# Gates and second shift and scale of an adaptive layer norm block, computed as columns on VectorE in place of products on TensorE

## Chip, core and metric

The kernel runs on one core of a Trainium2 chip. The metric is the device time of one execution in microseconds (us); the profile of one further execution shows where it goes. Everything is computed in float32.

## What is computed

Two samples of 1024 tokens and width 256 pass through one transformer block whose layer norms and residuals are modulated by a condition `c` (2 x 256):

```python
mod = (silu(c) @ wmod).reshape(2, 6, 1, 256)
sa, ca, ga, sb, cb, gb = (mod[:, i] for i in range(6))
ga = (2 * (ga >= 0) - 1) * maximum(abs(ga), 0.25)      # gb likewise
h = layernorm(x) * (1 + ca) + sa
x = x + ga * attention(h)       # 16 heads of 128, biases, rotary, causal softmax, Wo, bo
h = layernorm(x) * (1 + cb) + sb
x = x + gb * ffn(h)             # silu(gate) * up, 704 wide, weights dequantized, then down
```

So for each sample `wmod` gives six vectors of 256: shift, scale and gate of the attention block (`sa`, `ca`, `ga`) and of the feed-forward block (`sb`, `cb`, `gb`). The change touches how `ga`, `gb`, `sb` and `cb` are made. `sa` and `ca` are made as before.

## The kernel before

**Units and steps.** The main loop runs over 32 units, that is, heads: 16 heads of sample 0, then 16 of sample 1, two heads to a group (b, g, h). A unit n has eight steps i, one per row block of 128 tokens. The text calls unit n "head n". The order of the work on each engine is the order of the program, written out by hand under `manual_schedule`; each engine takes its instructions in order, and semaphores hold it up where it needs another's result.

In step i of head n the program issues: output products `py` of an earlier head (`shared_out`, lines 696 to 698, 13 row blocks behind) and their addition to `x` on VectorE (L521); the scores `ps` of row block i (L431) and, on VectorE, their masked negative maximum (L434, a fused add and minimum with an accumulator); the transposition of the row block before on VectorE (`turned`, L465), after every fourth of which SP issues 16 transfers `pT<-t` (L477); the exponential on ScalarE (L451); `release()`, which lets VectorE finish a half of the next head's q or k (L404). Then come, by step: projections of q and k for the next head (`project_qk`, L388, steps 1, 3, 4, 5), the values products of this group or the next (`project_v`, `pv`, L370, steps 0 and 2: two row blocks of 128 tokens each), the product of probabilities and values for the head before (`values`, `po`, L492; its first half at step 0, for heads 0 and 1 at step 2, its second half at steps 6 and 7), and `extras`, work that falls to particular steps.

**Values products.** A group's eight row blocks are made in four calls of `project_v`. For the first group all four lie in the prologue and in head 0. For every later group the first two calls lie in the second head of the group before, and the last two in its own first head. Their result goes through a PSUM tile and a ScalarE copy (L377).

**Buffers.** In PSUM, pool `ps_a` has two buffers (q and k projections, values products), `ps_o` one (`po`, values products of head 0), `ps_y` one (`py`, and of what concerns the change `pg` and the second `pm`), `ps_sc` two (scores). A q or k buffer in `ps_a` is free when ScalarE has read it (L400) and VectorE has finished L404, which is released a step later. In SBUF, `t32` holds the transposed blocks from which the 16 `pT<-t` transfers of a half are sent; VectorE can't overwrite a half before they have landed.

**Modulation.** `modulation(which, ...)` (L117) makes shift and scale of one block on TensorE: the weights are stationary, silu(c), repeated over 128 columns, is moving, and the results are columns (the 256 features on partitions), which is how they are needed. Block 0's runs at the start, block 1's at the end of step 7 of head 0 (L648). `shift_scale` (L136) copies them to `modT`, and adds 1 to the scale.

**Gates.** They are needed as rows, repeated over all partitions: `ga` is multiplied into the weights Wo of each group by GpSimd (`fold_out`, L332, first at the end of head 0), `gb` into the scales of the down projection (`ffn_down_scale`, head 8). `gates_product` (L146) multiplies silu(c), as stationary operand of two columns, with 512 columns of `wga`, in two calls of 256 inputs' halves in the prologue (L736 and L746). `gates` (L151), at L748 in the prologue, makes sign and magnitude of two rows of 512 on VectorE, writes them to DRAM (`grow_d`, two rows of 2 KB), and loads them back four times, repeated over 128 partitions.

**Queues.** SP issues nearly all transfers, in the program's order; a transfer that waits holds up those behind it. In the prologue it loads x, `wmod` for block 0, `wga`, the first weights, rotary tables, the rest of x, `wmod` for block 1, and the next group's weights. GpSimd's queue carries one transfer, `bo_bc`.

## Time and profile before

| what | before |
|---|---|
| median of 3 runs | 1075.6 us (1075.38 to 1075.73) |
| profiled execution, own time | 1076.84 us |
| its span | 1075.1 us |
| TensorE busy | 1070.5 us, 3529 instructions |
| VectorE busy | 655.1 us |
| ScalarE busy | 507.7 us |
| GpSimd busy | 396.1 us |
| DMA of SP and ACT queues | 49.4% and 1.2% of 16 engines' span |
| main loop begins, head 1, head 2, head 3 (first score on TensorE) | 25.11, 44.97, 72.54, 101.81 us |

Matmuls are pipelined, so a matmul's own duration is longer than its pitch, the time from its start to the next one's; TensorE's cost of a product is read from starts. An fp32 product takes two passes, which the trace shows as two instructions each. In the profile's groups and timelines a bracket or a last column names the idle time ahead of an instruction and what ended it. The chain of waits, followed back from the last instruction, says which engine the end of the run waited for.

### The profile page before, as it was taken

What the parts mean: (1) busy time and instruction counts of PE and PEld (TensorE: products, weight loads), DVE (VectorE), ACT (ScalarE), POOL (GpSimd) and SP (SyncE); (2) the same over time, 40 slices, a digit from 0 to 9 for tenths busy, and PEclk for the clock granted to TensorE, in tenths of its full rate; (3) what the DMA queues carried; (4) which work ended last, traced back from release to release, by engine and by line L of the source; (5) the groups of instructions that cost most, each with busy time, mean ns of one, the idle gap of its engine ahead of it and who ended that gap; (6) DMA issues with size and microseconds to landing.
All of it is one profiled execution on the core that took longest, in us unless ns stands there. A gap on an engine that the chain in (4) does not pass through costs nothing.

```text
span 1075.1 us, 12364 instructions
## 1 busy us (share of the span) xinstructions
PE 1070.5 (100%) x3529; PEld 641.4 (60%) x3529; DVE 655.1 (61%) x1423; ACT 507.7 (47%) x956; POOL 396.1 (37%) x364
## 2 busy tenths in 40 slices
PE   9999999999999999999999999999999999999998
PEld 5656555666666655555666656655555666555656
DVE  5656665666767776665666566666677765544421
ACT  4654544554445544544554444444454554562110
POOL 3825353534343343754332443324343433100000
PEclk9999999999999999999999999999999999999999
DMA  6465655657565555565554656454555556432001
GB/s 218 96 161 126 161 119 135 164 127 181 118 152 112 142 117 134 122 149 126 112 148 109 147 113 155 101 139 99 139 114 126 143 128 137 103 69 49 20 20 40
DMA packets 66656, 130.99 MB, mean 122 GB/s; under 512 B 18806, under 2 KB 22010, under 8 KB 66588
## 3 DMA queue, kind: packets, MB, share of 16 engines
q1 hardware_dynamic: 64804, 125.78, 49.4%
q10 hardware_dynamic: 1736, 4.29, 1.2%
q8 instruction: 29, 0.48, 0.2%
q14 instruction: 39, 0.32, 0.1%
q0 software_dynamic: 48, 0.13, 0.1%
HBM read 25.26 MB, written 2.10 MB: 25 GB/s over the span
## 4 chain that ended last, share of the span: by engine, by line
PE 99%; DMA 0%; DVE 0%; SPq 0%; issue 0%
PE po L492 23%; PE ps L431 23%; PE pv L370 10%; PE pq L388 10%; PE py L518 10%; PE pk L388 10%; PE pgu L547 7%; PE pd L606 3%; PE pm L125 1%; DMA wmod<-in_wmod 0%; PE pd L596 0%; PE ptx_a L218 0%; PE pg L149 0%; PE ptx_b L218 0%; PE pd_11r L606 0%; DVE x L521 0%
## 5 line engine op out<-in xcount | busy, mean ns | idle before, releaser
L451 ACT ACTIVATE p<-ps,nmax 128x128 f32<-128x128 f32 (+7 forms) x256 | 189.8, 741 | 342.7 <-DVE nmax L434 342.3
L431 PE MATMUL ps<-kT,qT 128*128 128x512 f32 (+3 forms) x768 | 289.5, 486 | 0.0
L434 DVE CUSTOM_DVE_ANT_0 ps<-ps,mask 128x128 f32<-128x128 f32 (+7 forms) x256 | 195.5, 764 | 114.5 <-PE ps L431 113.6
L492 PE MATMUL po<-pT,v 128*128 128x512 f32 (+3 forms) x768 | 263.7, 486 | 0.1
L521 DVE SCALAR_TENSOR_TENSOR x<-py,rden,x 128x256 f32<-128x256 f32 x256 | 122.7, 481 | 220.6 <-PE py L518 216.8
L492 PEld LDWEIGHTS po<-pT,v 128*128 128x128 f32 x768 | 145.7, 190 | 123.9 <-issue 92.8
L401 POOL TENSOR_TENSOR r_q<-r_q,sin_t 128x512 f32<-128x512 f32 x64 | 81.9, 1280 | 364.5 <-ACT r_q L400 348.9
L465 DVE STREAM_TRANSPOSE t<-p 128x128 f32<-128x128 f32 (+7 forms) x256 | 198.2, 774 | 3.6 <-DMA pT<-t 1.8
L431 PEld LDWEIGHTS ps<-kT,qT 128*128 128x128 f32 x768 | 145.7, 190 | 77.6 <-issue 64.1
L518 PE MATMUL py<-wo,o 128*128 128x256 f32 x512 | 151.2, 380 | 0.0
L518 PEld LDWEIGHTS py<-wo,o 128*128 128x128 f32 x512 | 92.6, 190 | 77.6 <-issue 53.1
L370 PE MATMUL pv<-wv,hT 128*128 128x256 f32 x512 | 121.1, 379 | 0.0
L388 PE MATMUL pq<-hT,wq 128*128 128x512 f32 x256 | 120.5, 593 | 0.0
L388 PE MATMUL pk<-hT,wk 128*128 128x512 f32 x256 | 120.3, 592 | 0.0
L370 PEld LDWEIGHTS pv<-wv,hT 128*128 128x128 f32 x512 | 94.8, 190 | 19.5 <-issue 1.3
L401 POOL TENSOR_TENSOR r_k<-r_k,sin_t 128x512 f32<-128x512 f32 x64 | 81.5, 1273 | 64.4 <-ACT r_k L400 64.4
L407 POOL TENSOR_TENSOR kT<-kT,r_k 128x512 f32<-128x512 f32 x64 | 81.2, 1269 | 55.8 <-DVE kT L404 41.1
L400 ACT ACTIVATE r_q<-pq,cols 64x512 f32<-64x512 f32 x128 | 87.4, 683 | 22.3 <-PE pq L388 19.8
L407 POOL TENSOR_TENSOR qT<-qT,r_q 128x512 f32<-128x512 f32 x64 | 83.7, 1308 | 33.9 <-DVE qT L404 29.7
L400 ACT ACTIVATE r_k<-pk,cols 64x512 f32<-64x512 f32 x128 | 87.4, 683 | 6.4 <-PE pk L388 1.0
L388 PEld LDWEIGHTS pk<-hT,wk 128*128 128x128 f32 x256 | 48.6, 190 | 48.0 <-issue 44.2
L388 PEld LDWEIGHTS pq<-hT,wq 128*128 128x128 f32 x256 | 46.2, 190 | 33.1 <-issue 30.6
(96 smaller groups left out, 691.3 us busy)
## 6 DMA issues: line engine op xcount, KB each, us to landing
pT<-t SPq DMA_DIRECT2D x512, 128.0 KB, 2.4
pT<-t SPq DMA_DIRECT2D x512, 64.0 KB, 2.0
wq<-in_Wq SPq DMA_DIRECT2D x16, 256.0 KB, 3.0
wk<-in_Wk SPq DMA_DIRECT2D x16, 256.0 KB, 4.1
wv<-in_Wv SPq DMA_DIRECT2D x16, 256.0 KB, 4.1
wo<-in_Wo SPq DMA_DIRECT2D x16, 256.0 KB, 2.9
out<-yo SPq DMA_DIRECT2D x15, 128.0 KB, 1.8
wmod<-in_wmod SPq DMA_DIRECT2D x4, 256.0 KB, 5.5
```

Source lines behind the costliest of these rows:

```text
L370: nc.tensor.matmul(pv[:, ts(j, HG * DH)], hT[b, n][:, k, ts(r, P)], weights[b, g]["v"][:, k, :], start=(k == 0), stop=(k == KC - 1),)
L388: nc.tensor.matmul(pq, weights[b, g][s][:, k, ts(h, DH)], hT[b, n][:, k, :], start=(k == 0), stop=(k == KC - 1),)
L400: nc.scalar.activation(r1[to], pq[of], AF.Identity, bias=cols[of, c : c + 1])
L401: nc.gpsimd.tensor_tensor(r1, r1, sin_t[:, sl], ALU.mult)
L407: nc.gpsimd.tensor_tensor(dst[:, sl], dst[:, sl], r1, ALU.add)
L431: nc.tensor.matmul(ps[:, c:e], qT[:, ts(i, P)], kT[:, c:e], start=True, stop=True)
L434: nc.vector.tensor_tensor_reduce(ps[:, :L], ps[:, :L], mask[:, NT - 1 - i :, :].rearrange("p t k -> p (t k)"), -SCALE, FLT_MAX, ALU.add, A ...
L451: nc.scalar.activation(p[:, :L], ps[:, :L], AF.Exp, bias=nmax, scale=-1.0, accum_out=dens[u][:, i : i + 1])
L465: nc.vector.transpose(t32[blk][:, :, j, : i + 1, :].rearrange("p c k b -> p k c b"), p[:, : (i + 1) * P].rearrange("p (k c a) -> p k c a", ...
L492: nc.tensor.matmul(po[:, off * P :], vs[b, g][:, k, ts(h, DH)], pT[:, off:, :, k, :], start=(k == 0), stop=(k == last),)
L518: nc.tensor.matmul(py[:, :D], outs[u][:, ts(t, P)], weights[b, g]["o"][:, h, :], start=True, stop=True)
L521: nc.vector.scalar_tensor_tensor(x[b][:, t, :], py[:, :D], rdens[u][:, t : t + 1], x[b][:, t, :], ALU.mult, ALU.add)
```

## The change

- `gates_product`, its weights `wga` and their load are gone, and so is the modulation of block 1 on TensorE. `modulation` now serves block 0 alone; it is called after `ln_scale`, and includes its two copies to `modT`.
- In their place `late_mod`, one buffer of the same pool, holds `wmT` (the weights of both gates and of block 1's shift and scale, transposed: output features on partitions, the 256 inputs along the row, 1 MB in two loads at the place of block 1's `wmod`) and `crow` (silu(c) of both samples as rows, repeated over all partitions).
- `crow` comes about at the start: ScalarE applies Silu to the row `row_c`, GpSimd's queue writes it to DRAM and loads it back repeated over the partitions.
- `column(which, n, f)` makes 128 features for both samples by one fused product and sum on VectorE each (`tensor_tensor_reduce` over 256 elements), into `gcol` or `modT`. `extras` calls it at steps 1 to 4 of head 0 (gates) and of head 1 (block 1's shift and scale): sixteen fused products in all.
- `gates` then works on 128 x 8 elements in place of 2 x 512, and moves from the prologue to step 4 of head 0. It writes its columns to `grow_d` so that they become rows there, and loads the rows back as before.
- The values products of the second group are all made in the first two heads: the first two calls at steps 6 and 7 of head 0, the other two at steps 0 and 2 of head 1. Head 2 has none. Later groups are as before.
- The first half of `values` moves from step 0 to step 2 in head 2, too.

```diff
-    wmod = fpool.tile([P, 2, 2, KC, D], F32, tag="f", name="wmod")
-    wga = fpool.tile([P, KC, 2 * D], F32, tag="f", name="wga")
+
+    wmod = fpool.tile([P, 2, KC, D], F32, tag="f", name="wmod")
+    late_mod = fpool.tile([P, (4 * KC + B) * D], F32, tag="f", name="late_mod")
+    wmT = late_mod[:, : 4 * KC * D].rearrange("p (w n f k) -> p w n f k", w=2, n=2, f=KC)
+
+    crow = late_mod[:, 4 * KC * D :].rearrange("p (b k) -> p b k", b=B)
...
-    def gates_product(k):
-        if k == 0:
-            pgs.append(ps_y.tile([P, 512], F32, tag="y", name="pg"))
-        nc.tensor.matmul(pgs[0][:B], sc[:, :, k], wga[:, k, :], start=(k == 0), stop=(k == KC - 1))
+    crow_d = dram.tile([1, B * D], F32, name="crow_d")
+    grow_d = dram.tile([B, 2, KC, P], F32, name="grow_d")
+    gcol = const.tile([P, B, 2, KC], F32, name="gcol")
+
+    def column(which, n, f):
+
+        junk = xnp.tile([P, D], F32, tag="xn", name=f"junk{which}{n}{f}")
+        for b in range(B):
+            to = modT[:, 2 + n, f, b : b + 1] if which else gcol[:, b, n, f : f + 1]
+            nc.vector.tensor_tensor_reduce(
+                junk, wmT[:, which, n, f], crow[:, b], 1.0, float(which * n), ALU.mult, ALU.add, to
+            )
 
     def gates():
 
-        pg = pgs.pop()
-        sgn = ppool.tile([P, S], F32, tag="p", name="sgn")[:B, :QB]
-        nc.vector.tensor_scalar(sgn, pg[:B], 0.0, 2.0, ALU.is_ge, ALU.mult)
...
+        g = gcol.rearrange("p b n f -> p (b n f)")
+        sgn = small.tile([P, 4 * B], F32, tag="sgn", name="sgn", bufs=1)
+        nc.vector.tensor_scalar(sgn, g, 0.0, 2.0, ALU.is_ge, ALU.mult)
...
-        nc.sync.dma_start(grow_d, mag)
+        with nc.allow_non_contiguous_dma("columns to rows"):
+            nc.sync.dma_start(grow_d.rearrange("b n f p -> p (b n f)"), mag)
         for b in range(B):
             for m, n in enumerate(("a", "b")):
                 nc.sync.dma_start(
-                    gate[n, b], grow_d[b : b + 1, m * D : (m + 1) * D].to_broadcast([P, D])
+                    gate[n, b],
+                    grow_d[b : b + 1, m].rearrange("b f p -> b (f p)").to_broadcast([P, D]),
                 )
...
-        if n == 0 and i == 7:
-            modulation(2, ps_y, "y")
-            shift_scale(2)
+
+        if n < 2 and 1 <= i <= 4:
+            column(n, *divmod(i - 1, 2))
+        if n == 0 and i == 4:
+            gates()
...
         nc.scalar.activation(sc.rearrange("p b k -> p (b k)"), pc[:, : B * KC], AF.Silu)
+        nc.scalar.activation(row_c, row_c, AF.Silu)
+        nc.gpsimd.dma_start(crow_d.rearrange("o (r p) -> (o r) p", p=P), row_c)
+        nc.gpsimd.dma_start(
+            crow.rearrange("p b k -> p (b k)"), crow_d.to_broadcast([P, B * D])
+        )
         nc.scalar.activation(warm, eps_t, AF.Sqrt)
         weights[0, 0] = {}
-        nc.sync.dma_start(wga, a["w_gates"])
...
         for n in range(2):
-            load_wmod(1, n, nc.sync)
+            nc.sync.dma_start(wmT[:, n], a["wmodT"][:, n])
...
-        modulation(0, ps_o, "o")
         ln_scale(0, "a", 0, (0, 1))
         ln_scale(0, "a", 0, (2, 3))
-        shift_scale(0)
+        modulation(ps_o, "o")
         ln_turn(0, "a", 0, 0, new_hT(0, 0), split=True)
-        gates_product(0)
...
         ln_turn(0, "a", 1, 0, new_hT(0, 1), split=True, wide=True)
-        gates_product(1)
         project_v(0, 0, 2, ps_sc, "sc", S)
-        gates()
...
+
                 if i in (0, 2):
-                    if h == 0:
-                        project_v(b, g, 4 + i, *((ps_a, "a") if n else (ps_o, "o")))
-                    elif more:
+                    if n < 2:
+                        project_v(b, n, 4 + i, *((ps_a, "a") if n else (ps_o, "o")))
+                    elif h == 0 and n > 2:
+                        project_v(b, g, 4 + i)
+                    elif h and more:
                         project_v(nb, ng, i)
+                if n == 0 and i in (6, 7):
+                    project_v(0, 1, 2 * (i - 6))
...
-                if prev and i == (0 if n > 1 else 2):
+                if prev and i == (0 if n > 2 else 2):
                     values(prev, 0, 0, 4)
```

More of the change, by code (lines that the diff above doesn't have):

```diff
@@ L58, in adaln_block, with load_wmod @@
     sc = const.tile([P, B, KC], F32, name="sc")
-    wmod = fpool.tile([P, 2, 2, KC, D], F32, tag="f", name="wmod")
-    wga = fpool.tile([P, KC, 2 * D], F32, tag="f", name="wga")
+    wmod = fpool.tile([P, 2, KC, D], F32, tag="f", name="wmod")
+    late_mod = fpool.tile([P, (4 * KC + B) * D], F32, tag="f", name="late_mod")
+    wmT = late_mod[:, : 4 * KC * D].rearrange("p (w n f k) -> p w n f k", w=2, n=2, f=KC)
+    crow = late_mod[:, 4 * KC * D :].rearrange("p (b k) -> p b k", b=B)
     def load_x(b, t, n, eng):
         eng.dma_start(x[b][:, t : t + n, :], x_d[b, :, t : t + n, :])
-    def load_wmod(block, n, eng):
-        eng.dma_start(wmod[:, block, n], a["L0_wmod"][block, n])
+    def load_wmod(n, eng):
+        eng.dma_start(wmod[:, n], a["L0_wmod"][n])
     row_c = rot.tile([P, QB], F32, tag="r1", name="row_c")[: B * KC, :P]
@@ L76, in adaln_block @@
     for n in range(2):
-        load_wmod(0, n, nc.sync)
+        load_wmod(n, nc.sync)
     ident = const.tile([P, P], F32, name="ident")
@@ L115, in adaln_block, with modulation @@
     bvacc = const.tile([P, D], F32, name="bvacc")
-    def modulation(which, pool, tag):
-        pm = pool.tile([P, 512], F32, tag=tag, name=f"pm{which}")
+    def modulation(pool, tag):
+        pm = pool.tile([P, 512], F32, tag=tag, name="pm")
         wide = pm.rearrange("p (n f r b) -> p n f r b", n=2, f=KC, b=B)
@@ L126, in modulation @@
                         wide[:, n, f],
-                        wmod[:, which // 2, n, k, ts(f, P)],
+                        wmod[:, n, k, ts(f, P)],
                         sc[:, :, k].unsqueeze(1).to_broadcast([P, P // B, B]),
@@ L131, in modulation @@
                     )
-        pms[which] = wide
-    pms = {}
-    def shift_scale(which):
-        pm = pms[which]
         for n in range(2):
-            nc.vector.tensor_scalar(modT[:, which + n], pm[:, n, :, 0, :], float(n), None, ALU.add)
+            nc.vector.tensor_scalar(modT[:, n], wide[:, n, :, 0, :], float(n), None, ALU.add)
     dram = pool("dram", 1, space=bass.MemoryType.DRAM)
-    grow_d = dram.tile([B, 2 * D], F32, name="grow_d")
-    pgs = []
-    def gates_product(k):
-        if k == 0:
-            pgs.append(ps_y.tile([P, 512], F32, tag="y", name="pg"))
-        nc.tensor.matmul(pgs[0][:B], sc[:, :, k], wga[:, k, :], start=(k == 0), stop=(k == KC - 1))
-    def gates():
-        pg = pgs.pop()
-        sgn = ppool.tile([P, S], F32, tag="p", name="sgn")[:B, :QB]
-        nc.vector.tensor_scalar(sgn, pg[:B], 0.0, 2.0, ALU.is_ge, ALU.mult)
-        mag = ppool.tile([P, S], F32, tag="p", name="mag")[:B, :QB]
-        nc.vector.tensor_scalar(mag, pg[:B], -1.0, None, ALU.mult)
-        nc.vector.scalar_tensor_tensor(mag, pg[:B], 0.25, mag, ALU.max, ALU.max)
+    crow_d = dram.tile([1, B * D], F32, name="crow_d")
[8 more added lines that the diff above has]
+            )
+    def gates():
+        g = gcol.rearrange("p b n f -> p (b n f)")
+        sgn = small.tile([P, 4 * B], F32, tag="sgn", name="sgn", bufs=1)
+        nc.vector.tensor_scalar(sgn, g, 0.0, 2.0, ALU.is_ge, ALU.mult)
+        mag = small.tile([P, 4 * B], F32, tag="mag", name="mag", bufs=1)
+        nc.vector.tensor_scalar(mag, g, -1.0, None, ALU.mult)
+        nc.vector.scalar_tensor_tensor(mag, g, 0.25, mag, ALU.max, ALU.max)
         nc.vector.scalar_tensor_tensor(mag, sgn, -1.0, mag, ALU.add, ALU.mult)
-        nc.sync.dma_start(grow_d, mag)
+        with nc.allow_non_contiguous_dma("columns to rows"):
+            nc.sync.dma_start(grow_d.rearrange("b n f p -> p (b n f)"), mag)
         for b in range(B):
@@ L875 @@
     wmod = v["L0_wmod"].reshape(D, 2, 3, D)
-    args["L0_wmod"] = given("in_wmod", by_partition(np.moveaxis(wmod[:, :, :2], 0, 2), 2))
-    args["w_gates"] = given("in_w_gates", by_partition(wmod[:, :, 2].reshape(D, 2 * D)))
+    args["L0_wmod"] = given("in_wmod", by_partition(np.moveaxis(wmod[:, 0, :2], 0, 1), 1))
+    wmT = np.stack([wmod[:, :, 2], wmod[:, 1, :2]]).reshape(2, D, 2, KC, P)
+    args["wmodT"] = given("in_wmodT", wmT.transpose(4, 0, 2, 3, 1))
     gate, up, down = (v[f"L0_ffn_wq_{n}"].T for n in ("gate", "up", "down"))
```

## The prediction

> **What bounds the kernel now.** I read the page first, then the chain of work in order of time, then the timeline of each engine around the places that the diff touches.

> ```profile
> PE 1070.5 (100%) x3529; PEld 641.4 (60%) x3529; DVE 655.1 (61%) x1423; ACT 507.7 (47%) x956; POOL 396.1 (37%) x364
> ...
> PE 99%; DMA 0%; DVE 0%; SPq 0%; issue 0%
> PE po L492 23%; PE ps L431 23%; PE pv L370 10%; PE pq L388 10%; PE py L518 10%; PE pk L388 10%; PE pgu L547 7%; PE pd L606 3%; PE pm L125 1%; DMA wmod<-in_wmod 0%; PE pd L596 0%; PE ptx_a L218 0%; PE pg L149 0%; PE ptx_b L218 0%; PE pd_11r L606 0%; DVE x L521 0%
> ```

> TensorE is the bound: 99% of the chain lies on it. From 11 us on its matmuls start at an even pitch (0.43 us per pass of 512 columns, two passes per product), and until head 31 hardly anything holds one up. So a matmul that goes from the chain is worth its pitch, and work added to another engine costs nothing until a matmul waits for it. The diff takes two lines from the chain: pm (L125), of whose 1% one half is at the start, and pg (L149).

> ```profile
> 40.12 3.22 PE ps L431 x8
> 43.34 1.78 PE pm L125 x16
> 45.35 1.73 PE pv L370 x8
> ```

> The second modulation is here in full: in the timeline it starts at 43.18 and head 1's first score at 44.97, 1.79 us.

> ```profile
> 11.39 0.81 DVE L226 TENSOR_SCALAR hT<-ptx_a,modT 128x512 f32<-128x512 f32 x1 [0.58 <-PE ptx_a L218]
> 11.71 1.02 PE L149 MATMUL pg<-wga,sc 128*2 128x512 f32 x2
> ...
> 12.66 1.98 PE L388 MATMUL pq<-hT,wq 128*128 128x512 f32 x4
> ...
> 18.89 1.02 PE L149 MATMUL pg<-wga,sc 128*2 128x512 f32 x2
> ...
> 19.84 1.99 PE L370 MATMUL pv<-wv,hT 128*128 128x256 f32 x8
> ```

> The two gates products differ. The second lies between ready matmuls (18.89 to 19.84). The first fills a hole: the product behind it needs hT, which VectorE finishes only at 11.39 + 0.81 = 12.20.

> [...] the masked scores of 256 columns (L434) took 0.40 to 0.43 us, each with an accumulator read of 0.13. [...] the trace shows the half rate only before 11.18 (213 ns, then 109 ns, per 128 columns). [...]

> **The change part by part.**

> *Start.* Without the first pg, pq starts when hT is there, at 12.20 plus about 0.06 for the semaphore (below): 12.26 for 12.66, −0.4. Its second half of hT, ScalarE's 11.82 + 0.78 = 12.60, is in time. The second pg gives −0.95, up to −1.15 if the slower first pv behind it (0.32 for 0.22) goes too; I take −1.0. What follows stays fed: hT's second block follows the transposes on VectorE and ScalarE, which have 1.7 us of pv as cover. Sum −1.4, bounds −0.9 (first pg worth nothing) to −1.6. wga (512 KB) leaves SP's queue behind wmod, so wmod, which TensorE waits for until 6.79, doesn't come sooner. The row's Silu is one small ACT instruction (0.2 us) ahead of the square root's table, which then ends near 5.4; its first use is at 6.64. POOL gets two DMAs ahead of its memsets and waits for the first to land; it then works until about 9.5 and is next needed at 16.33: hidden. wmT adds 0.5 MB to SP's early queue, where wga took 0.5 MB away: wo, the last in it, landed at 19.0 and is needed after 45.

> *Second modulation.* −1.79. With it 2 VectorE copies of 0.1 go.

> *Values products.* Two pv of 1.73 us (8 passes of 0.216) enter head 0 at steps 6 and 7, those of head 1 are exchanged for the next two, and head 2 loses two: +3.46, 0, −3.46. At the end of head 0 the pv takes pm's place as the cover under the last row's maximum and exponential; it is as long. In head 2, however, nothing is left between the first steps' output products:

> ```profile
> 72.10 0.60 PE L518 MATMUL py<-wo,o 128*128 128x256 f32 x2
> 72.54 0.38 PE L431 MATMUL ps<-kT,qT 128*128 128x128 f32 x2
> 72.76 1.89 PE L370 MATMUL pv<-wv,hT 128*128 128x256 f32 x8
> 74.49 2.32 PE L492 MATMUL po<-pT,v 128*128 128x512 f32 x8
> 76.64 0.60 PE L518 MATMUL py<-wo,o 128*128 128x256 f32 x2
> ```

> pv goes and po moves to step 2, so the next py follows the first score directly, 0.66 after the first py. Pool ps_y has one buffer, which VectorE's addition (L521) must have emptied. The tail of the run shows this very sequence:

> ```profile
> 932.34 0.59 PE L518 MATMUL py<-wo,o 128*128 128x256 f32 x2
> 932.77 0.81 PE L431 MATMUL ps<-kT,qT 128*128 128x384 f32 x2
> 933.51 0.70 PE L518 MATMUL py<-wo,o 128*128 128x256 f32 x2
> ```

> There the addition ran from 932.97 to 933.45, and the next py began at 933.51, 1.17 us after the first, and 0.1 slower in its own first pass. In head 2 that is 1.17 − 0.66 + 0.1 = +0.6 (0.4 to 0.9). The pT that po needs then comes later on SP (below), but po is 4 us later too.

> *Columns.* Sixteen fused products, eight in each of heads 0 and 1, two per step: 2 × (0.42 + 0.05) and a wait between them, 0.95 us a step, and four tiny operations at step 4, 0.6 together. VectorE is busy for 13.2 of 20 us in head 0. Of the steps, the tightest is the last:

> ```profile
> 35.43 0.83 DVE L434 CUSTOM_DVE_ANT_0 ps<-ps,mask 128x640 f32<-128x640 f32 x1 [1.61 <-PE ps L431]
> ...
> 36.81 0.71 DVE L404 SCALAR_TENSOR_TENSOR kT<-pk,cols,cos_t 128x512 f32<-128x512 f32 x1
> 38.44 0.97 DVE L434 CUSTOM_DVE_ANT_0 ps<-ps,mask 128x768 f32<-128x768 f32 x1 [0.92 <-PE ps L431]
> ...
> 40.09 0.71 DVE L404 SCALAR_TENSOR_TENSOR qT<-pq,cols,cos_t 128x512 f32<-128x512 f32 x1
> ```

> Step 3's columns fit into the 1.61 us of idling. Step 4's run from 37.5 to 39.05 with the four small ones, so the maximum comes 0.6 late, and qT's release of its ps_a buffer ends at 41.4 for 40.8 (times of before). Step 6's new pv wants that buffer at 41.45. I charge +0.1 (0 to 0.5). ps itself has two buffers and a whole step's slack. Head 1's steps have more room (2.67 and 1.61 us of idling at steps 3 and 4): 0. In exchange VectorE's four row operations at 19.95 (2.7 us) go; nothing waited for them.

> *Gates' transfers.* They move from SP's idle time to behind head 0's first sixteen pT, and what is queued behind them is sixteen more.

> ```profile
> 22.68 0.31 SPq L160 DMA_DIRECT2D grow_d<-mag  x1
> 23.98 0.36 SPq L163 DMA_DIRECT2D ga<-grow_d  x1
> ...
> 36.95 29.51 SPq L477 DMA_DIRECT2D pT<-t  x43
> ```

> SP issues a pT every 0.63 us without a rest. grow_d took 1.25 from issue until the load behind it could go; now it has 1024 elements of 4 bytes, 64 to each of 16 DMA engines. In the packet records a semaphore's 4 bytes took 9 ns, a row of 192 bytes 15, one of grow_d's 2 KB rows 125. So the wait is 1.7 to 9.2 us; I take 15 ns, 64 × 15 = 1.0, and 2.2 in all. Then, with 1.4 us gained at the start: first sixteen issued by 47.05 − 1.4 = 45.7, grow_d landed 47.9, four loads 1.8 to 49.7, the next pT from 49.7 to 59.2, landing 2.4 later, 61.6. TensorE wants them at 64.36, VectorE's next transposition (L465, which reuses t) at 61.80; head 1 itself shifts by −1.4 − 1.79 + 3.46 + 0.1 = +0.37, so 64.7 and 62.2: cost 0. The cover is gone from a wait of 2.2 + 3.1 = 5.3 us on. POOL gets ga near 51 for 28, and its product with wo waits 2 us; it idles 4.46 us afterwards: 0.

> **Sum.** −1.4 − 1.79 + 0.6 + 0.1 = −2.5. The profiled execution was 1076.84 with a span of 1075.1, its span so 1072.6; the median of the three runs shown, 1075.6, becomes 1073.1 (−0.23%).

> **Rivals.** *VectorE becomes late in head 0*: if a column costs 0.85 instead of 0.47, step 2's pair delays the next row's maximum by 1.3, step 3's adds as much, pk waits 0.7 and pv 1.5, giving back 2.2: 1075.3. For it: in-order VectorE and two ps_a buffers; against it: the 256-column row above. *SP's round trip, moderate*: a wait of 7 us holds po in head 1 for 7 − 5.3 = 1.7: 1074.8. *The same, dear (slower)*: [...] po waits 11.9: 1085. It turns slower than before above 5.3 + 2.5 = 7.8 us, and by over 0.2% above 10. Against it: 4-byte writes of 9 ns. *The removed matmuls were free*: no, their successors started at once.

> **Chances.** Differences within 0.2% (2.15 us) are about what a measurement of this kernel can't tell from none. Forecast with its bounds (1072.4 to 1073.9): 0.70, of which 0.56 below 1073.45. VectorE late: 0.11. Round trip moderate: 0.10, partly above 1075.6. Dear: 0.07. Something better still: 0.02. Together: faster 0.58, same 0.35, slower 0.07. The range for 8 in 10 is 1072.3 to 1075.4: it covers the forecast and most of the two middle cases, and leaves out the dear one.

> **What would show it.** Right: no pg, pq at 12.3; head 0's first score near 23.7; head 1 beginning near 45.3; one gap of about half a microsecond on TensorE before head 2's second py, ended by x (L525 then); head 3 starting about 2.5 earlier. Wrong: TensorE waiting for pT or for qT in heads 0 and 1, gates' loads on SP later than 50, or columns above 0.6 us each.

## The result, and the profile after

| | before | after |
|---|---|---|
| median of 5 runs each, taken together | 1075.73 us | 1085.26 us (1083.28 to 1086.78) |
| profiled execution, own time | 1076.84 us | 1085.26 us |
| its span | 1075.1 us | 1083.5 us |
| TensorE busy, instructions | 1070.5 us, 3529 | 1069.7 us, 3509 |
| VectorE busy | 655.1 us | 666.1 us |

After / before is 1.0082, with a 95% interval of 1.0071 to 1.0092: the kernel became 0.8% slower, where 0.23% faster was forecast. The two profiled executions differ by 8.4 us; the medians by 9.5, because the profiled execution of before lies 1.1 us above its median.

TensorE has less work than before, and still the end comes later. The chain of waits (part 4 of the page of the changed kernel) says so at once: 99% TensorE has become 96%, and names that weren't there have come in.

```profile
PE 96%; DVE 2%; DMA 1%; ACT 1%; issue 0%; SPq 0%; ACTq 0%; DVEq 0%
PE po L496 23%; PE ps L435 22%; PE py L522 10%; PE pq L392 10%; PE pv L374 10%; PE pk L392 10%; PE pgu L551 7%; PE pd L610 3%; DVE junk L149 1%; DMA wmod<-in_wmod 0%; PE pd L600 0%; DMA pT<-t 0%; DVE ps L438 0%; ACT r_k L404 0%; DVE t L469 0%
```

`junk` (L149) is the column operation, `pT` the transposed probabilities. Where the time went can be read from the start of each head's first score on TensorE, worked out stretch by stretch:

| stretch | forecast | measured, after minus before | what is in it |
|---|---|---|---|
| up to head 0 | -1.4 | -2.64 (25.11 to 22.47) | 1.0 to 1.4 of it is no effect of the change, see below |
| head 0 | +1.77 | +7.11 | waits of 0.9 and 2.7, then half clock |
| head 1 | 0 | +6.37 | waits of 0.2 and 4.3, then half clock |
| head 2 | -2.86 | -2.77 | as forecast |
| the rest | 0 | +0.34 | |
| sum | -2.5 | +8.41 | |

From head 3 to head 31 the two runs stay in step: the whole loss arises within 60 us. TensorE's timeline of the changed kernel has both holes; the bracket is the idle time ahead and what ended it. It counts from the end of the matmul before; counted by starts, that is, against the start that an even stream would have had, a wait is about 0.16 us longer. The waits named in this text are counted by starts.

```profile
36.50 1.98 PE L392 MATMUL pk<-hT,wk 128*128 128x512 f32 x4 [0.73 <-DVE kT L408]
...
42.48 3.27 PE L374 MATMUL pv<-wv,hT 128*128 128x256 f32 x8 [2.50 <-DVE qT L408]
...
47.72 1.89 PE L374 MATMUL pv<-wv,hT 128*128 128x256 f32 x8
...
73.43 5.37 PE L496 MATMUL po<-pT,v 128*128 128x512 f32 x8 [4.11 <-DMA pT<-t]
...
84.21 0.67 PE L522 MATMUL py<-wo,o 128*128 128x256 f32 x2 [0.45 <-DVE x L525]
```

Read the durations too. The eight matmuls of `pv` take 1.89 us at 47.72, where the second modulation stood, and 3.27 at 42.48; `po` takes 5.37 at 73.43, and 3.60 at the same place in head 1 of before:

```profile
64.36 3.60 PE L492 MATMUL po<-pT,v 128*128 128x512 f32 x8
```

Behind each of the two long holes TensorE ran at half its clock. The table by stretches gives the granted clock third from the end, 0.50 in both:

```profile
43.04:46.45 3.41, 3.41 (x9) 2.32 (x8) 1.92 (x4) 2.24 (x4) 3.33 (x4) 0.50 0.40 100
...
73.76:77.17 3.41, 3.41 (x5) 1.35 (x4) 3.41 (x6) 0.70 (x1) 2.04 (x2) 0.50 0.33 79
```

3.41 us at half the clock lose 1.7 each. So head 0's excess over the forecast, 5.3, is 0.9 + 2.7 + 1.7, and head 1's, 6.4, is 0.2 + 4.3 + 1.7, each to within 0.2.

**The first hole: VectorE.** Its timeline in head 0, and GpSimd's of the same microseconds, side by side:

```profile
26.17 2.70 DVE L149 CUSTOM_DVE_ANT_0 junk<-late_mod 128x256 f32<-128x256 f32 x1
...
28.91 0.42 DVE L149 CUSTOM_DVE_ANT_0 junk<-late_mod 128x256 f32<-128x256 f32 x1
...
31.19 1.36 DVE L149 CUSTOM_DVE_ANT_0 junk<-late_mod 128x256 f32<-128x256 f32 x1
...
38.58 1.11 DVE L157 TENSOR_SCALAR sgn<-gcol 128x8 f32<-128x8 f32 x1
```

```profile
26.08 1.28 POOL L411 TENSOR_TENSOR qT<-qT,r_q 128x512 f32<-128x512 f32 x1
27.30 1.27 POOL L411 TENSOR_TENSOR kT<-kT,r_k 128x512 f32<-128x512 f32 x1
28.92 1.55 POOL L405 TENSOR_TENSOR r_q<-r_q,sin_t 128x512 f32<-128x512 f32 x1 [0.34 <-ACT r_q L404]
30.96 1.31 POOL L411 TENSOR_TENSOR qT<-qT,r_q 128x512 f32<-128x512 f32 x1 [0.49 <-DVE qT L408]
...
38.22 1.44 POOL L405 TENSOR_TENSOR r_q<-r_q,sin_t 128x512 f32<-128x512 f32 x1
```

A column took 0.42 us where it started ahead of GpSimd (28.91 against 28.92). Those that started under a GpSimd operation ended some 0.3 us after one. Seven of the sixteen did so, and the other nine took 0.38 to 0.43. Four of the seven met two GpSimd operations without a gap between them: one ended after both (26.08 and 27.30, the second ending at 28.58), at 28.87, and three (at 37.17, 60.67 and 63.94) after the first alone. Even 128 x 8 elements took 1.11, under a GpSimd operation that ended at 39.66. So a column took 0.38 to 0.43 us, or 0.77 to 2.70.

**The second hole: SP.** Its timeline and, of the same stretch, the part on transfers (GB/s in 40 slices of 0.2 us; the last column of an issue is the time to its landing):

```profile
46.07 0.53 SPq L163 DMA_DIRECT2D grow_d<-mag  x1
54.81 0.34 SPq L166 DMA_DIRECT2D ga<-grow_d  x1
...
56.70 5.34 SPq L481 DMA_DIRECT2D pT<-t  x6
```

```profile
GB/s 80 210 30 5 7 7 2 0 0 0 0 0 0 0 0 0 0 0 0 0 100 190 190 150 170 160 220 80 20 0 0 0 0 0 0 0 0 0 0 0
...
grow_d<-mag SPq DMA_DIRECT2D x1, 4.0 KB, 8.7
```

The load behind `grow_d` could go 8.7 us after it. The small packets themselves were over within the first seven slices, 1.4 us; the traffic in the middle is a load on ScalarE's queue. What SP waited for, 8.2 us of the 8.7 by its list of waits, is the completion of writes that had long been sent. The next `pT` left SP at 56.70, the last of the sixteen at 68.25; TensorE had wanted them at 69.2 and went on at 73.43.

**The start.** `pm` took 2.02 us for sixteen matmuls, in place of 3.75, since TensorE's full clock came at 5.5 us instead of 11.2. The onset varies from run to run: 4.6 to 11.2 us in the profiles of this study, with the same first matmuls. In the kernels below whose onset was late as well, at 10.8 to 11.1 (experiments 2, 4 and 10), head 0 began 1.72, 1.59 and 1.61 earlier than before. The kernel before itself, with an early onset at 5.5 and 5.9, began head 0 at 23.73 and 23.69 (experiments 8 and 12, whose additions come later), 1.4 earlier than in its own profile; against these the changed kernel's 22.47 is 1.2 earlier, and its variants below with an early onset are 0.7 to 1.4 earlier. So the change's own effect is 0.7 to 1.7, and the rest of the 2.64 is the onset.

### The profile page after: what moved, and what is told of

The parts are those of the page before. It is cut to its first block, busy times and chain, and to the rows that moved or that the text cites. A ratio compares the mean times of both kernels' runs of the same rounds, so it can differ in the third digit from the quotient of the medians.

```text
span 1083.5 us, 12352 instructions
## 1 busy us (share of the span) xinstructions
PE 1069.7 (99%) x3509; PEld 638.6 (59%) x3509; DVE 666.1 (61%) x1453; ACT 508.9 (47%) x957; POOL 398.5 (37%) x366
## 4 chain that ended last, share of the span: by engine, by line
PE 96%; DVE 2%; DMA 1%; ACT 1%; issue 0%; SPq 0%; ACTq 0%; DVEq 0%
PE po L496 23%; PE ps L435 22%; PE py L522 10%; PE pq L392 10%; PE pv L374 10%; PE pk L392 10%; PE pgu L551 7%; PE pd L610 3%; DVE junk L149 1%; DMA wmod<-in_wmod 0%; PE pd L600 0%; DMA pT<-t 0%; DVE ps L438 0%; ACT r_k L404 0%; DVE t L469 0%
## 5 line engine op out<-in xcount | busy, mean ns | idle before, releaser
L525 DVE SCALAR_TENSOR_TENSOR x<-py,rden,x 128x256 f32<-128x256 f32 x256 | 122.6, 480 | 217.8 <-PE py L522 214.0
L405 POOL TENSOR_TENSOR r_k<-r_k,sin_t 128x512 f32<-128x512 f32 x64 | 81.5, 1274 | 61.7 <-ACT r_k L404 61.6
L404 ACT ACTIVATE r_q<-pq,cols 64x512 f32<-64x512 f32 x128 | 87.6, 684 | 22.5 <-PE pq L392 19.2
L404 ACT ACTIVATE r_k<-pk,cols 64x512 f32<-64x512 f32 x128 | 87.6, 684 | 6.3 <-PE pk L392 1.0
```

What stands on the lines that cost most here:

```text
L404: nc.scalar.activation(r1[to], pq[of], AF.Identity, bias=cols[of, c : c + 1])
L405: nc.gpsimd.tensor_tensor(r1, r1, sin_t[:, sl], ALU.mult)
L525: nc.vector.scalar_tensor_tensor(x[b][:, t, :], py[:, :D], rdens[u][:, t : t + 1], x[b][:, t, :], ALU.mult, ALU.add)
```

## The experiments

All times are medians; each was compared with runs of the kernel before on the same chip, whose medians were 1075.9 to 1076.2. Experiments 8 and 12 are single executions.

**1. The columns' second operand from PSUM.** ScalarE copies the row of silu(c) into the bank of `ps_y`, which is free until the first `py`; nothing else differs.

```diff
+    crow_ps = ps_y.tile([P, 512], F32, tag="y", name="crow_ps")
...
+        nc.scalar.copy(crow_ps, crow.rearrange("p b k -> p (b k)"))
...
-                junk, wmT[:, which, n, f], crow[:, b], 1.0, float(which * n), ALU.mult, ALU.add, to
+                junk, wmT[:, which, n, f], crow_ps[:, ts(b, D)], 1.0, float(which * n), ALU.mult, ALU.add, to
```

> The changed kernel, but ScalarE copies the row of c into a PSUM bank (free until head 1's step 5) and the sixteen column operations read it from there; number, order and length of VectorE's work are as before. Theory 1 (two stalls in series: [...] grow_d's element-wise write holds SP): all columns 0.38 to 0.50 us, none above 0.6; TensorE's waits of 0.9 and 2.7 us ahead of pk and pv in head 0 and the half clock at 43 us go, so head 1 starts 4 to 5 us earlier; but pT of head 0's second block still hangs on SP, which begins with the first sixteen only some 1.5 us earlier, so po in head 1 waits some 7 to 8 us instead of 4.3: in all 1083 to 1084, hardly faster than 1085.3. Rival A (the columns are simply VectorE work of 0.4 us and more that fits nowhere): columns still 0.7 us in the mean, head 0 as long as in the changed kernel, 1085. Rival B (the columns alone are to blame, SP is hidden): 1078 to 1080.

Measured: 1083.86, ratio 1.0074 (1.006 to 1.0087). The line of the column operation, first of the changed kernel, then of this one (duration in ns: least, median, longest):

```profile
L149 DVE CUSTOM_DVE_ANT_0 junk<-late_mod x16: 376/426/2697, 26.2 to 65.0; 128x256 f32<-128x256 f32 x16
```

```profile
L149 DVE CUSTOM_DVE_ANT_0 junk<-late_mod,crow_ps x16: 381/414/422, 26.2 to 60.3; 128x256 f32<-128x256 f32 x16
```

VectorE has the same instructions in the same order, and no long one is left: the second SBUF operand under GpSimd was the cause, not the amount of work. Head 1 began 4.1 us earlier, and `po` in head 1 then waited 5.4 in place of 4.3, still for `pT`. So most of the gain was given back, as theory 1 said and rival B did not. Two parts of the expectation missed. `po` waited 5.4 us and not 7 to 8, since 1.5 of the wait now lay ahead of it, at the first `py` of head 1 (experiment 3 has that wait too). And `pv` in head 0 still waited 1.2 us. The four small operations on the gates, which still have SBUF operands only, explain it:

```profile
35.75 0.60 DVE L157 TENSOR_SCALAR sgn<-gcol 128x8 f32<-128x8 f32 x1
...
36.46 1.12 DVE L160 SCALAR_TENSOR_TENSOR mag<-gcol,mag 128x8 f32<-128x8 f32 x1
```

They lie under GpSimd's operations of 35.06 to 36.33 and 36.29 to 37.55, and took 1.95 us up to the start of the next operation, for 0.57 in experiment 10, where they meet none.

**2. The gates written by rows.** TensorE transposes the 128 x 8 gates at step 5 of head 0, ScalarE copies the 8 x 128, and SP writes them in the same place of its queue; the columns stay in SBUF.

```diff
-            nc.sync.dma_start(grow_d.rearrange("b n f p -> p (b n f)"), mag)
...
+        nc.tensor.transpose(pr[: 4 * B, :P], mag, ident)
...
+        nc.scalar.copy(rows, pr[: 4 * B, :P])
+        nc.sync.dma_start(grow_d.rearrange("b n f p -> (b n f) p"), rows)
```

> The changed kernel, columns from SBUF as there, but the gates' 128x8 are transposed by TensorE at head 0's step 5 and written to DRAM as 8 contiguous rows of 512 bytes, in the same place of SP's queue. Theory 1: the wait on SP behind the write falls from 8.7 to about 2 us, the four loads land within 4 us, pT of head 0's second block is issued 7 us earlier, po's wait in head 1 (4.3) and the half clock behind it (1.7) go; head 0 keeps its stalls: 1085.3 - 6.2 = 1079 (1078 to 1080). Rival A (the loads behind the write, or the sixteen pT themselves, are what is slow): the loads still take 6 us to land and po still waits 3 us or more: 1083 to 1085. Rival B (only the columns count): 1085.

Measured: 1078.04, ratio 1.0016 (1.0008 to 1.0025), at the low end of what theory 1 gave.

```profile
47.00 0.47 SPq L173 DMA_DIRECT2D grow_d<-rows  x1
48.53 0.35 SPq L176 DMA_DIRECT2D ga<-grow_d  x1
```

1.5 us in place of 8.7 with the same 4 KB. The loads landed in about 4 us, and `po` in head 1 waited for nothing. The second hole hung on the form of this one write. In head 0 the wait came divided, 2.0 ahead of the transposition and 0.56 ahead of `pv`, and its half clock didn't come either.

**3. Both edits.**

> Both edits: the row of c in PSUM and the gates written by rows. Theory 1: head 0's stalls (0.9 + 2.7 and 1.7 for the half clock) and head 1's (4.3 + 0.2 and 1.7) all go: 1085.3 - 11.4 = 1073.8 (1073 to 1075), faster than before by about what was forecast for the change. If one of the two were an effect of the other, the gain of both would be that of one alone, 1079 to 1083. If TensorE's clock falls whatever the stalls, 1.7 or 3.4 us stay: 1076 to 1077.

Measured: 1077.57, ratio 1.0013 (1.0007 to 1.002): much of the loss gone, but not 1073.8. The clock didn't fall in its profile. The profiled execution took 1076.13. TensorE's timeline shows three other waits: 1.5 us ahead of `py` at step 5 of head 1 (for VectorE: the bank of `ps_y` still holds the row for the columns of step 4), 0.57 ahead of the transposition of the gates, which is placed too early, and 0.56 ahead of `pv` at step 6 of head 0. The first two are the price of my repairs.

**4. As 3, with `values` of head 2 back at step 0.**

> Both edits, and in head 2 the first output products of the values (po) go back to step 0, between the first two py: the wait of py for the one buffer of ps_y (0.6 us) should go, since pT is in time once SP is not held: 0.5 to 0.7 below the kernel with both edits, near 1073.2. Rival: po in step 0 waits for pT itself or for ps_o, and nothing or less than nothing is won.

Measured: 1077.54, ratio 1.0009 (1.0002 to 1.0015), no gain: the rival held. `py` no longer waits for `ps_y`, but `po` now follows the `po` of head 1 too closely and waits 0.5 for ScalarE to empty `ps_o`, which has one buffer as well.

**5. As 3, with the three waits removed:** head 1's columns at steps 0 to 3, the transposition at step 6, the `pv` of step 6 in `ps_o`.

> Both edits (row of c in PSUM, gates by rows), with the three waits removed that the kernel with both edits showed on TensorE: head 1's columns one step earlier (steps 0 to 3), so that the first py doesn't wait 1.5 us for the bank that holds the row; the gates' transposition at step 6 behind the values product (it waited 0.57 for the gates); the values product of step 6 in ps_o (it waited 0.56 for ps_a). Theory 1: the three waits, 2.65 us, go: 1077.6 - 2.65 = 1074.9 (1074.3 to 1075.6). Rival: they only stood in for other waits (kT or qT of head 1, the buffers of ps_sc) and 1 us or less is won: above 1076.5.

Measured: 1074.76, ratio 0.9985 (0.9977 to 0.9992). Theory 1 to within 0.2; faster than before, by 0.15%.

**6. As 5, with one values product ahead instead of two,** and the transposition in `ps_o` again.

```diff
+                        project_v(b, n, (2 if n else 4) + i, *((ps_a, "a") if n else (ps_o, "o")))
+                    elif n == 2 and i == 0:
+                        project_v(b, g, 6)
...
-                if n == 0 and i in (6, 7):
-                    project_v(0, 1, 2 * (i - 6))
+                if n == 0 and i == 7:
+                    project_v(0, 1, 0)
```

> As the kernel with both edits and the three waits removed, but only one values product is moved ahead: one at head 0's step 7, the next two in head 1, the last at head 2's step 0, so that head 2's second py has cover. Theory 1: the wait of py in head 2 (0.6 us) goes as well: 0.6 below that kernel, near 1074.3. Rival: the product in head 2 waits for its weights, its buffer or hT: no difference.

Measured: 1074.32, ratio 0.9976 (0.9966 to 0.9986). The wait of `py` in head 2 is gone from the trace, but without a `pv` at step 6 the last score of head 0 waits 0.9; the difference from 5 is within the intervals.

**7. Only half of the element-wise write in head 0**, on the changed kernel: gate a's 512 elements, gate b's at the end of head 1.

```diff
+            nc.sync.dma_start(
+                grow_d[m].rearrange("b f p -> p (b f)"), gates_mag[0][:, ts(m, 2 * B)]
+            )
```

> The changed kernel, but only the 512 elements of gate a are written by grow_d's element-wise transfer in head 0 and loaded behind it; gate b's 512 follow at head 1's end and are loaded in head 2. Theory 1a (the transfer costs by the element, 8.7 us / 1024 = 8.5 ns each): the loads behind it go 4.4 us after its issue, and po in head 1 waits hardly at all: about 6 us below the changed kernel, 1079. Theory 1b (such a transfer has a fixed completion of some 8 us, whatever its elements): the loads go 8 us or more after it, and the time stays at 1084 to 1085.

Measured: 1089.55, ratio 1.0122 (1.0107 to 1.0137). Half the elements took 8.3 us for 8.7: 1a falls. The run is slower even than 1b says, because the second such write, issued at 76.95, landed 9.5 us later, and everything behind it on SP with it: a weight load issued at 77.58 landed at 89.3, the next `pT`, of 80.49, at 92.7. `po` in head 3 waited 5.3 for them.

**8. Forms of small writes, measured by themselves**, on the kernel before, on ScalarE's queue in heads 16 to 27.

> The kernel before, with 24 writes added to DRAM that nobody reads, on ScalarE's DMA queue in heads 16 to 27: six forms in turn, four times each: 1024 elements of 4 bytes turned (like grow_d), 128 turned, 16 turned, 1024 and 128 with each element in its own 64 bytes, and 128 of 32 bytes. To be read: time from issue to landing. If the cost is by the element: 1024 take 8 us, 128 take 1 to 2, 16 about 1.5. If it is fixed for a write of single elements: all forms of 4 bytes take 8 us. If it is from elements that share a 64-byte line[...]: 1024 turned, 128 turned and perhaps 16 turned are slow, the ones apart about 2 us. The run's time: within 1 us of before.

Time from issue to landing, where the trace has it:

| form (4-byte elements, but for the last) | us |
|---|---|
| 1024, neighbours in DRAM, as `grow_d` | 10.6, 10.9, 10.3, 10.8 |
| 128, neighbours (512 bytes in all) | 6.7, 6.7 |
| 16, neighbours (64 bytes in all) | 1.7, 1.6 |
| 1024, each in its own 64 bytes | 3.1, 3.8, 3.1, 4.1 |
| 128, each in its own 64 bytes | 1.7, 1.7 |
| 128 of 32 bytes, neighbours | 1.9, 2.0, 1.9, 2.0 |

Neither by the element (1024 spread out are three times as fast as 1024 side by side) nor fixed. What was slow here are many 4-byte writes side by side: 6.7 us for 128, 10.3 to 10.9 for 1024. The third guess has this order right, but by its reason the 16 that share 64 bytes should be slow too, and they are not. In the trace the parts of a write of 128 neighbours completed one after another, from 1.5 to 6.7 us after the issue, those of 128 apart all between 1.5 and 1.7, and those of `grow_d` in the changed kernel between 7.4 and 8.7. Why they complete so late isn't shown. That the time passes after the packets shows again in the stretch from 491.9 to 502 (busy tenths of the DMA engines in 40 slices):

```profile
DMA  8696920000000000000000000000000000000000
```

The run took 1099.14, where I expected no difference. SP issued a `pT` at 490.82, and the next only at 502.06, when the write on ScalarE's queue, issued at 491.4, had landed 10.6 us later. From 480 to 610 five of SP's waits ended with such a write, 28.6 us in all, the longest 10.6: transfers slow to complete on one queue stopped another. In this program the two queues share their completion semaphores: in the trace of before, the 1155 transfers of SP and the 13 of ScalarE use the same eight.

**9. As 6, with the values products and `values` of head 2 where the kernel before has them.**

> As the kernel with both edits and the three waits removed, but with all values products of the second group, and the values of head 2, where the kernel before has them; so nothing stands at the end of head 0 where the second modulation stood. If the removed modulation was real work on the path: 1074.3, like the kernel with one product moved. Rival (the modulation was only cover there, and head 1 can't start sooner): TensorE waits up to 1.8 us at the end of head 0, and the time is 1075 to 1076.

Measured: 1075.78, ratio 0.9995 (0.9986 to 1.0003), 1.5 us above 6. TensorE waits 0.9 ahead of head 0's last score, as in 6, and then 0.8 and 0.6 more at the start of head 1, each time for ScalarE, which empties the scores' buffers with its exponentials; the wait of 0.8 ended with its copy of the gates' rows (0.24 us), which belongs to the repair. The rival held for most of it: the second modulation was work on the path, but also the cover of these exponentials. Taken away without a `pv` in its place it brings little.

**10. As 6, with head 0's columns and the gates' small operations one step earlier.**

> As the kernel with one values product moved, but head 0's columns and the gates' small operations one step earlier (steps 0 to 3), since that kernel still shows a wait of 0.89 us on TensorE ahead of head 0's last score. If that wait is VectorE's lateness from the columns of steps 3 and 4 (the row 'columns' of the forecast): it shrinks below 0.3 and the time falls by 0.6 to 0.9, to 1073.5. Rival: the same lateness appears one step earlier, or comes from elsewhere: 1074.3.

Measured: 1074.32, ratio 0.9982 (0.9975 to 0.9989). The wait of 0.9 is gone: from the prologue's end to head 31 the trace shows no wait on TensorE above 0.15. Its full clock came at 11.06, as in the profile of before, and its span is 2.9 below that one's. The median is that of 6, though: the rival's number, and the gain of 0.6 to 0.9 that was expected doesn't show.

**11. As 5, with the values products spread:** two at the end of head 0, one in head 1, one at head 2's step 0.

> As the kernel with both edits and the three waits removed, with values products at head 0's steps 6 and 7 as there, then one in head 1 and the last at head 2's step 0. Cover both at head 0's end and in head 2: the wait of py in head 2 (0.6) goes: 1074.8 - 0.6 = 1074.2. Rival: head 1 is now 1.7 us shorter ahead of its products of pT, which lands too late for po: a new wait of up to 1 us, 1075.

Measured: 1073.76, ratio 0.9978 (0.9968 to 0.9987), the lowest median; its interval overlaps those of 5, 6 and 10. The wait in head 2 is gone, and the rival's wait is there: 0.7 ahead of `po` in head 1, for `pT`.

**12. Holes of known length on TensorE**, on the kernel before.

```diff
+        nc.scalar.copy(idle, one[:, :P])
+        for _ in range(3 * (n % 6)):
+            nc.scalar.copy(idle, idle)
+        two = ps_y.tile([P, 512], F32, tag="y", name=f"two{n}")
+        nc.tensor.matmul(two[:, :P], ones, idle, start=True, stop=True)
```

> The kernel before, with a hole on TensorE added at step 2 of heads 4 to 27 (a product whose operand ScalarE copies over and over: none, 3, 6, 9, 12 or 15 copies), so holes of about 0.5 to 4 us, four of each. [...] If a hole of about 2.5 us is enough, as in the changed kernel: every hole from 2.5 us on is followed by 3.41 us of half clock (1.7 us lost), those below 1.5 us by none[...].

The run took 1221.46, at a mean granted clock of 0.954. Holes of 0.8 us were followed by no drop of the clock (4 of 4); of 1.8 and of 2.8 by 3.41 us at half clock (7 of 7); of 3.6 and more by 6.83 us, begun within the hole (13 of 13). One of 1.8 us (1.61 in the bracket), and a product behind it that ran partly at half clock; at full clock it takes 1.88:

```profile
462.27 0.49 PE L706 MATMUL two<-idle,ones 128*128 128x128 f32 x2 [1.61 <-ACT idle L704]
...
465.08 2.71 PE L388 MATMUL pk<-hT,wk 128*128 128x512 f32 x4
```

The holes that count are shorter than the 2.5 us that I expected: 1.8 us were enough here, 2.7 in the changed kernel. All half-clock stretches here are 3.41 us or twice that. In the changed kernel's trace the full clock came at 5.49 and the half clock at 43.04 and 73.76, that is 37.55 and 68.27 us after the onset, 11.0 and 20.0 times 3.41.

Length alone doesn't decide. In experiment 2 a hole of 2.0 (ahead of the transposition) was not followed by a drop. The holes of 4.3 in the changed kernel and 5.4 in experiment 1 brought 3.41 us, not 6.83. So I laid bins of 3.41 us end to end from the onset of the full clock and counted TensorE's idle share in each, by the brackets, over all traces that have the clock. In experiment 8's trace two holes lasted 3.0 us: one lay within a single bin and was followed by 3.41 us at half clock, the other was divided between two bins and by none. In the changed kernel the bins from 39.63 and from 70.35 were idle for 73% and 90%, and a bin at half clock followed each; the one from 66.94, idle for 32%, was followed by the full clock. At full clock, each of the 24 bins that were idle for 67% or more was followed by one at half clock, and none of the 24 with 20% to 43%. From 49% to 54% it went both ways: four bins of this run were followed by a drop, one each of experiments 1, 2 and 8 was not. A bin at half clock was followed by a second one where the hole ran on into it for 21% of it or more (14 of 14), and by the full clock otherwise.

## Why the prediction was wrong, step by step

All three of the signs that the prediction named for being wrong came: TensorE waited for `qT` in head 0 and for `pT` in head 1, the gates' loads went at 54.81, and columns took up to 2.70 us.

- **Start, -1.4: right.** 1.6 to 1.7 with a late onset of the clock on both sides, 0.7 to 1.4 with an early one on both; the bounds were -0.9 and -1.6. The rest in the profile is the onset's chance.
- **Second modulation, -1.79, and values products, +3.46, 0, -3.46: right.** Head 2 came out at -2.77 for -2.86. What the two holes hide in heads 0 and 1 shows in experiment 5: 2.1 more than before for +1.77 in head 0, and no difference in head 1. Experiment 9 adds what the text said in passing: the `pv` has to take the modulation's place as cover.
- **`py` in head 2, +0.6: right.** 0.61 in the trace.
- **Columns, "I charge +0.1 (0 to 0.5)": failed.** It cost 5.3 us in head 0 with the small operations and the clock; 4.1 of it went in experiment 1. The term was 0.47 us a column, with the masked scores (L434) as its measure. For a column that meets no GpSimd operation this was right, 0.38 to 0.43 and an accumulator read of 0.08. What failed is that nothing was charged for waiting on GpSimd. The row of the masked scores reads one operand from PSUM; the columns read both from SBUF. A row of the same engine, length and kind wasn't the same kind in what decided it. The trace of before did show such waiting, in the layer norm's scaling, which reads SBUF alone, takes 0.41 us, and sometimes three times as long:

```profile
L204 DVE TENSOR_SCALAR xn_a<-x,mv_a,rstd_a x16: 406/412/1225, 7.8 to 382.2; 128x256 f32<-128x256 f32 x16
```

  At 346.12 and 375.39, for example, it took 1.2 us, starting 0.2 after GpSimd had begun a rotary product of 1.27. The rival "VectorE becomes late" had the right chain (maximum, `pk`, `pv`), but a smaller price, and no clock in it.
- **Gates' transfers, "I take 15 ns ... and 2.2 in all": failed.** 8.7 us, within the bound of 1.7 to 9.2 that stood beside it. The step that failed is the price by the packet: the packets were quicker than estimated (7 to 9 ns each), the completion was not. From 5.3 us on, the text said, the cover is gone; 8.7 makes 3.4, and 4.3 was measured. That the two are close is chance. TensorE came to this `po` 4.5 us later than forecast (69.2 for 64.7), mostly through the first hole, which should have hidden the write; but the sixteen `pT` took 11.6 us to issue in place of 9.5, and the last landed about 5 us after its issue in place of 2.4. So the rival "moderate" was the right mechanism; its 7 us would have had to be 8.7, with the slower `pT` and the clock added. The "dear" rival's 1085 is the measured time by luck alone: it had `po` wait 11.9 us, where 4.3 was measured, and knew nothing of the first hole or of the clock.
- **Clock, at nothing: failed.** That the change's holes leave the clock alone was the author's estimate; no trace had yet shown what a hole does to it. A hole of 0.6 (0.47 in the bracket, at 10.64) indeed cost nothing, but holes of 2.7 and 4.3 each brought 1.7 us on top of their own length.
- **The sum.** With both causes removed, the sign and over half of the forecast come out: 1.4 us faster than before, for 2.5, with the wait in head 2 (experiment 5), and 1.7 to 2.2, for 3.1, without it (10, 6 and 11). The two profiles with a late onset, of experiment 10 and of before, differ by 2.9.

What stays open: why neighbouring 4-byte writes complete so late, and what decides for a bin that TensorE leaves idle for about half.

## What to carry to other kernels

Before moving work to an engine that is "half idle", look at where its operands lie and at what runs beside it: for VectorE beside a busy GpSimd, one operand in PSUM was the difference between 0.42 and up to 2.70 us. Price a transfer by its completion and by what is queued behind it, not by its packets (8.7 us against 1.4 here), and turn columns into rows on TensorE rather than by 4-byte writes (1.5 us in place of 8.7 for the same 4 KB). Count for a hole in TensorE's stream more than its length: those of 2.7 and 4.3 us here each cost 1.7 us again. And with two holes in series, a repair of the first alone may only lengthen the second: it won 1.4 us (experiment 1), the repair of the second alone 7.2 (experiment 2).
